# An MLP in two parts of its inner width, squares a step ahead, and two tiles given up, in a four-layer network

## The chip, the cores and the metric

The kernel runs on one core of a Trainium2 chip. The metric is device time in microseconds for one execution, in which the core computes all four layers for the whole batch of 8 images. The time before is the median of three runs, 7783.18 us (7766.74 to 7798.79).

TensorE is called PE in the profile (PEld its weight loads), VectorE is DVE, ScalarE is ACT, GpSimd is POOL, and SyncE is SP, whose queue issues every transfer of this kernel.

## The reference

The input is 8 images of 384 channels and 32 x 32 pixels in float32. Four layers follow each other, and each adds its result to its input, which a group norm (32 groups of 12 channels) has scaled before:

```python
x = x + L0(_gn(x))   # selective scan ("Mamba") over the 1024 pixels
x = x + L1(_gn(x))   # 1x1 conv, 8x8 FFT filter, 3x3 depthwise, gelu gate, 1x1 conv
x = x + L2(_gn(x))   # layer norm, selective scan, then an MLP 384 -> 1536 -> 384
x = x + L3(_gn(x))   # 3x3 depthwise conv
```

The scan is the core of L0 and L2. For 768 inner channels d and 16 states n it runs over the pixels t:

```python
dt = softplus(dt @ dt_proj_w.T + dt_proj_b)
h  = exp(dt_t * A) * h + (dt_t * u_t) * B_t      # for each d and n
y  = sum_n(h * C_t) + u * D
y  = y * silu(z);  out = y @ out_proj_w.T
```

L2 puts a layer norm ahead of the scan and, behind its output projection, `gelu(t @ mlp_w1.T + b1) @ mlp_w2.T + b2`.

## The kernel before

An image is cut into two chunks of T = 512 pixels, so that each scan layer has 16 chunks. A chunk's 768 channels times 16 states are 96 scans of 128 partitions by 512 pixels, taken four at a time: 24 steps a chunk (`QUADS`, channel block k of 6, part sub of 4), 768 steps in all. The main loop walks over the steps. In step t it issues

- `times` (L623): POOL multiplies the tile g of step t + 1 (dt*u, spread over states) by B;
- `scan` (L643 to L660): DVE runs four scans; two end in PSUM and DVE multiplies them by C (L654), two end in g and POOL multiplies them by C (L660);
- `gather` of step t - 1: PE sums over states into y with `sely`. With the last sub of a block it adds u*D (in L0 by a matmul with the diagonal matrix w_D, in L2 by DVE, L678) and multiplies by the gate z (L681);
- `begin` of step t + 3 (L613): SP loads g, 1 MB, from a DRAM copy `dud` of dt*u, once `gather` has freed one of four g tiles;
- `decay` of step t + 1: PE spreads dt over states into the four PSUM tiles dA, and ACT takes their exp (L241).

All other work is cut into pieces (Python generators run by `Jobs`), and it is put between these. `begin` of `Jobs` gives each step a budget of TensorE and VectorE time (`ROOM`), `step` takes pieces by due time while they fit, and `until` forces pieces, in order of due time, until a condition holds. A piece yields NEXT if it goes on in the next step, EARLY if its next piece is to open a step, WAIT if it can't go on. The jobs that matter here:

- `measure`: loads six blocks xk of an image (tile `spm`, two buffers) for the group norm's statistics. `live["spm"]` is True meanwhile.
- `front`: loads xf, normalizes it, in L2 runs `layer_norm`, then the in-projection, the short convolution, dbc, and `step_dt` for six blocks d. `layer_norm` waits until `live["spm"]` is False, and then, k by k in one piece, ACT writes the square sq (tile `spm`) and PE sums it into ps_lv.
- `step_dt`: PE makes ps_dt; ACT makes a softplus part m in tile `spm` by Abs, Exp and Ln; DVE adds it up to dt (L85); a step later POOL multiplies dt by u into tile du (L583, two buffers), and SP spills du into `dud` in four transfers (L590). The loop over d waits while seven dt tiles live or `live["spm"]` is True; a unit that has begun is carried on when the loop comes round.
- `finish`: the output projection, then in L1's place `layer1`, or for L2 the `mlp`, and after the image's second chunk `layer3`.
- `mlp`: for each half of the chunk's pixels (256), `up` makes 12 blocks of the inner width from t, in units of two blocks that share a PSUM tile, Gelu runs over h1, and `down` makes three output blocks, each the sum over all 12. The weights come as pieces of 384 KB (tile mw, four buffers, L889), each loaded for each half, so 24 pieces a chunk. A piece is loaded when a later one is taken.

PE executes in the order of the program: matmuls of jobs, of `gather` and of `decay` share one queue, as all transfers share SP's. The lines L177 (matmul), L241 (activation) and L85 (metered DVE operation) are helpers, so the groups are told apart by tile names.

Of the kernel before, what the change touches and what calls it, by code (L numbers as in the profile page):

```python
# [10 lines left out]
F32 = mybir.dt.float32  # L11
AF = mybir.ActivationFunctionType
ALU = mybir.AluOpType
# [40 lines left out]
def _flat(ap):  # L54
    return ap.rearrange("p a b -> p (a b)")
# [100 lines left out]
def tile_conv_preact_d4(ctx: ExitStack, tc: tile.TileContext, a: dict, out: bass.AP):  # L156
# [10 lines left out]
    live = {"ps": 0, "dt": 0, "x": 0, "spm": False}  # L167
    work = [0.0, 0.0]
    jobs = Jobs(work)
    vector = Meter(nc.vector, work, 1)  # L170
# [182 lines left out]
        vector.tensor_scalar_mul(w["A"], w["A"], -1.0)  # L353
        return w

    def load_diagonal(w, pre):
        w["D"] = wk.tile([P, ND, P], F32, tag="w_D", name="w_D")
        nc.sync.dma_start(w["D"], a[pre + "D"].rearrange("d p q -> p d q"))
# [40 lines left out]
    def measure(s):  # L399

        blocks = [(h, k) for h in range(2) for k in range(KC)]
        loaded = {}

        def load(q):
            if q < len(blocks):
                h, k = blocks[q]
                x = loaded[h, k] = wk.tile([P, T], F32, tag="spm", name="xk", bufs=2)
                nc.sync.dma_start(
                    x, s["src"][s["b"], k * P : (k + 1) * P, h * T : (h + 1) * T]
                )  # L410

        live["spm"] = True
        load(0)
        load(1)
        yield NEXT

        def block(h, k):
            return loaded.pop((h, k)), lambda: load(blocks.index((h, k)) + 2)

        def all_read():  # L420
            live["spm"] = False

        s["stats"] = yield from group_stats(block, all_read, NEXT)

# [35 lines left out]
    def layer_norm(xn):  # L460
        ps = yield from ps_tile("ps_ln")
        for k in range(KC):
            mm(ps, ln_mean, xn[:, k, :], start=k == 0, stop=k == KC - 1)
        for k in range(KC):
            vector.tensor_sub(xn[:, k, :], xn[:, k, :], ps)
        ps_done()
        yield NEXT
        while live["spm"]:
            yield WAIT
        ps = yield from ps_tile("ps_lv")  # L470
        for k in range(KC):
            sq = wk.tile([P, T], F32, tag="spm", name="sq", bufs=2)
            act(sq, xn[:, k, :], AF.Square)
            mm(ps, ln_mean, sq, start=k == 0, stop=k == KC - 1)
        rsqrt(ps, ps, eps_ln)
        yield
        for k in range(KC):
            vector.scalar_tensor_tensor(
                xn[:, k, :], xn[:, k, :], ln_w[:, k : k + 1], ps, ALU.mult, ALU.mult
            )  # L480
        ps_done()
        yield NEXT
        for k in range(KC):
            act(xn[:, k, :], xn[:, k, :], AF.Identity, bias=ln_b[:, k : k + 1])
        yield NEXT

    def front(s):
# [78 lines left out]
        def step_dt(d):  # L566
            got = {}


            def log(ps):  # L570
                mm(ps, w["dt"][DT0:RX, d * P : (d + 1) * P], dbc[DT0:RX, :])
                v = got["m"] = wk.tile([P, T], F32, tag="spm", name="spm", bufs=2)
                act(v, ps, AF.Abs)
                act(v, v, AF.Exp, scale=-1.0)
                act(v, v, AF.Ln, bias=1.0)

            def plus(ps):
                v = s["dt"][d] = wk.tile([P, T], F32, tag="dt", name="dt", bufs=NDT)
                vector.scalar_tensor_tensor(v, ps, 0.0, got["m"], ALU.max, ALU.add)

            def times_u(ps):
                v = got["du"] = wk.tile([P, T], F32, tag="du", name="du", bufs=2)
                nc.gpsimd.tensor_mul(v, s["dt"][d], u[d])  # L583

            def spill(ps):
                to = s["dud"][d] = dram.tile(
                    [NSUB * E8, 4, T], F32, tag="dud", name="dud", bufs=2 * ND
                )
                for j in range(4):
                    nc.sync.dma_start(to[:, j, :], got["du"][32 * j : 32 * (j + 1), :])  # L590

            return [both(log, plus), None, both(times_u, spill)]

        yield from pipe([("ps_bc", [spread(j)]) for j in range(2)])
        yield
        flying = []
        for d in range(ND):
            while live["dt"] >= NDT or live["spm"]:
                yield WAIT
            live["dt"] += 1  # L600

            flying.append(pipe([("ps_dt", step_dt(d))]))
            flying = [f for f in flying if next(f, f) is not f]
            yield NEXT
        while flying:
            flying = [f for f in flying if next(f, f) is not f]
            yield NEXT


    def begin(s, i):  # L610
# [53 lines left out]
    def gather(s, i):  # L664
# [5 lines left out]
        g = s.pop(("g", i))  # L670
        for j in range(4):
            mm(y[32 * j : 32 * (j + 1), :], sely[:, sub, :], g[:, j, :], sub == 0, sub == NSUB - 1 and s["pre"] == "l2_")
        if sub == NSUB - 1:
            u = s["u"][k // NH][:, k % NH, :]
            if s["pre"] == "l0_":
                mm(y, s["w"]["D"][:, k, :], u, start=False)
            else:
                nc.vector.scalar_tensor_tensor(  # L678
                    y, u, s["w"]["vec"][:, k, 4:5], y, ALU.mult, ALU.add
                )  # L680
            nc.vector.tensor_mul(u, y, s["z", k // NH][:, k % NH, :])  # L681
            if k == NH - 1:
                s["half"] = True
# [175 lines left out]
        s["done"] = True  # L859


    TH = T // 2
    NFH = NF // 2
    xp = None

# [6 lines left out]

    def weights():

        parts = [a["l2_mlp_w1"][f : f + 2].rearrange("f p k q -> p f k q") for f in range(0, NF, 2)]
        parts += [
            a["l2_mlp_w2"][m][:, g * NFH : (g + 1) * NFH, :]
            for m in range(KC)
            for g in range(2)
        ]  # L880
        parts = deque(parts + parts)
        loaded = deque()

        def more():
# [11 lines left out]
    def mlp(s):  # L896
        x = s["x"]
        loaded, more = s["weights"]
        first = True

        def take():

            nonlocal first
            if not first:
                more()
            first = False
            return loaded.popleft()

        for half in range(2):
            cols = slice(half * TH, (half + 1) * TH)  # L910
            h1 = p2.tile([P, NF, TH], F32, tag="h1", name="h1")

            def up(f):
                def run(q):
                    def run_q(ps):
                        if q == 0:
                            now[0] = take()
                        cols_q = slice(q * TH, (q + 1) * TH)
                        for k in range(KC):
                            mm(  # L920
                                ps[:, cols_q], now[0][:, q * KC + k, :],
                                s["t"][k][:, cols], start=k == 0, stop=k == KC - 1,
                            )

                    return run_q

                def evict(ps):
                    for q in range(2):
                        act(
                            h1[:, f + q, :], ps[:, q * TH : (q + 1) * TH], AF.Identity,  # L930
                            bias=b1[:, f + q : f + q + 1],
                        )

                now = [None]
                return [run(0), both(run(1), evict)]

            yield from pipe([("ps_up", up(f)) for f in range(0, NF, 2)], deep=1)
            yield EARLY
            for q in range(2):
                part = _flat(h1[:, q * NFH : (q + 1) * NFH, :])  # L940
                act(part, part, AF.Gelu)
            exp_again()
            yield NEXT

            def down(m):
                def sum_up(g, third):
                    def run(ps):
                        if third == 0:
                            now[0] = take()
                        for f in range(third * KC, (third + 1) * KC):  # L950
                            mm(
                                ps[:, :TH], now[0][:, f, :], h1[:, g * NFH + f, :],
                                start=g == 0 and f == 0, stop=g == 1 and f == NFH - 1,
                            )

                    return run

                now = [None]

                def add(ps):  # L960
                    xc = x[:, m, cols]
                    vector.scalar_tensor_tensor(
                        xc, ps[:, :TH], b2[:, m : m + 1], xc, ALU.add, ALU.add
                    )
# [214 lines left out]
```

## Time and profile before

| | us |
|---|---|
| median of three runs | 7783.18 |
| the profiled execution | 7774.96 |
| its span | 7773.2 |
| PE busy | 7244.1 |
| DVE busy | 5787.0 |
| POOL busy | 5638.8 |
| ACT busy | 4034.0 |
| mean granted TensorE clock | 0.922 |

The span is the time from the first to the last instruction of one profiled execution. An engine's busy time counts an instruction from its start to its end, and a matmul that waits or runs at a low clock in between counts as busy too. A row of the groups names the line, the engine, the operation, the tiles written and read, the shape and the count; then come the busy time, the mean of one in ns, and the idle time just before such instructions with what ended it. A row of the waits has the waiting instruction, the one it waited for, the total in us, the number of times and the longest.

The first layer's steps last until about 3552 us, where the first scan of the third layer (the one with the MLP) begins. From about 7590 us on no scan is left, and the last chunk's output projection, MLP and depthwise convolution run alone.

### The profile page before, as it was taken

What the parts mean: (1) busy time and instruction counts of PE and PEld (TensorE: products, weight loads), DVE (VectorE), ACT (ScalarE), POOL (GpSimd) and SP (SyncE); (2) the same over time, 40 slices, a digit from 0 to 9 for tenths busy, and PEclk for the clock granted to TensorE, in tenths of its full rate; (3) what the DMA queues carried; (4) which work ended last, traced back from release to release, by engine and by line L of the source; (5) the groups of instructions that cost most, each with busy time, mean ns of one, the idle gap of its engine ahead of it and who ended that gap; (6) DMA issues with size and microseconds to landing.
All of it is one profiled execution on the core that took longest, in us unless ns stands there. A gap on an engine that the chain in (4) does not pass through costs nothing. (4 is left out here: it accounts for less than half of the span.)

```text
span 7773.2 us, 76689 instructions
## 1 busy us (share of the span) xinstructions
PE 7244.1 (93%) x25762; PEld 3001.0 (39%) x25762; DVE 5787.0 (74%) x7350; ACT 4034.0 (52%) x6980; POOL 5638.8 (73%) x2710
## 2 busy tenths in 40 slices
PE   7989999999999999999999989999999999999998
PEld 2223333333333333333334434444444444444445
DVE  5988788888777878778746765767777677776871
ACT  4445555554554555455545544555555555555543
POOL 5888878788787878778646764767767677676770
PEclk8888889999888999988899999999999999999999
DMA  5666556556565646556536654666656666565662
GB/s 141 141 151 144 138 134 142 136 135 150 127 146 127 141 120 148 128 139 146 129 78 167 174 135 120 165 156 172 165 150 174 155 170 164 149 164 146 171 168 67
DMA packets 288919, 1122.50 MB, mean 144 GB/s; under 512 B 37386, under 2 KB 90970, under 8 KB 190220
## 3 DMA queue, kind: packets, MB, share of 16 engines
q1 hardware_dynamic: 288524, 1117.59, 58.4%
q8 instruction: 204, 3.34, 0.2%
q14 instruction: 191, 1.56, 0.1%
HBM read 1041.96 MB, written 75.50 MB: 144 GB/s over the span
## 5 line engine op out<-in xcount | busy, mean ns | idle before, releaser
L623 POOL TENSOR_TENSOR g<-g,bc 128x1024 f32<-128x1024 f32 x1536 | 3586.8, 2358 | 197.2 <-DMA g<-dud 181.2
L660 POOL TENSOR_TENSOR g<-g,bc 128x1024 f32<-128x1024 f32 x768 | 1806.2, 2352 | 1441.1 <-DVE carry L656 806.6
L241 ACT ACTIVATE dA<-dA,w_A 128x512 f32<-128x512 f32 x3072 | 1860.7, 662 | 1543.3 <-PE dA L177 1530.1
L177 PE MATMUL dA<-dt,selr 32*128 32x512 f32 x6144 | 1573.3, 677 | 70.6 <-DVE g L654 61.9
L643 DVE TENSOR_TENSOR_SCAN dA<-dA,carry,g 128x512 f32<-128x512 f32 x768 | 986.6, 1285 | 616.0 <-issue 275.6
L643 DVE TENSOR_TENSOR_SCAN dA<-dA,g 128x512 f32<-128x512 f32 x768 | 940.6, 1225 | 477.5 <-issue 167.7
L654 DVE TENSOR_TENSOR g<-dA,bc 128x512 f32<-128x512 f32 x1536 | 1053.9, 686 | 29.8 <-DVE dA L643 0.5
L177 PE MATMUL y<-g,sely 128*32 128x512 f32 x6144 | 934.1, 637 | 43.0 <-POOL g L660 37.5
L643 DVE TENSOR_TENSOR_SCAN g<-dA,carry,g 128x512 f32<-128x512 f32 x768 | 940.6, 1267 | 0.0
L643 DVE TENSOR_TENSOR_SCAN g<-dA,g 128x512 f32<-128x512 f32 x768 | 893.3, 1204 | 0.0
L177 PEld LDWEIGHTS dA<-dt,selr 32*128 32x128 f32 x6144 | 470.2, 191 | 984.4 <-DVE g L643 517.3
L177 PE MATMUL ps_dn<-h,mw 128*128 128x256 f32 x2304 | 573.9, 401 | 75.3 <-DMA mw<-in_l_mlp_w 58.6
L177 PE MATMUL ps_up<-t,mw 128*128 128x256 f32 x2304 | 566.8, 394 | 59.0 <-DMA mw<-in_l_mlp_w 44.2
L177 PE MATMUL ps_z<-xf,w_in 128*128 128x512 f32 x1152 | 586.1, 649 | 27.3 <-DVE dt L85 23.6
L177 PE MATMUL ps_in<-xf,w_in 128*128 128x512 f32 x1152 | 566.9, 633 | 27.3 <-DVE u L85 25.5
L177 PE MATMUL ps_dw<-tp,diag 96*96 96x512 f32 x1152 | 572.8, 638 | 15.2 <-ACT diag L241 15.2
L177 PE MATMUL ps_out<-u,w_out 128*128 128x512 f32 x1152 | 543.7, 619 | 10.2 <-DVE x L85 10.2
L177 PEld LDWEIGHTS ps_dn<-h,mw 128*128 128x128 f32 x2304 | 439.5, 197 | 277.0 <-issue 118.8
L177 PEld LDWEIGHTS ps_up<-t,mw 128*128 128x128 f32 x2304 | 425.8, 192 | 268.4 <-issue 148.9
L177 PE MATMUL ps_dw<-xp,diag 128*128 128x512 f32 x864 | 407.5, 622 | 42.2 <-ACT diag L241 40.9
L241 ACT ACTIVATE u<-ps_in,w_vec 128x512 f32<-128x512 f32 x192 | 149.4, 778 | 484.2 <-PE ps_in L177 484.2
L177 PEld LDWEIGHTS y<-g,sely 128*32 128x32 f32 x6144 | 134.2, 111 | 648.5 <-issue 461.1
(99 smaller groups left out, 6463.1 us busy)
## 6 DMA issues: line engine op xcount, KB each, us to landing
g<-dud SPq DMA_DIRECT2D x768, 1024.0 KB, 7.1
mw<-in_l_mlp_w SPq DMA_DIRECT2D x384, 384.0 KB, 7.4
dud<-du SPq DMA_DIRECT2D x768, 64.0 KB, 1.7
xk<-in_x SPq DMA_DIRECT2D x48, 256.0 KB, 4.2
xf<-in_x SPq DMA_DIRECT2D x16, 768.0 KB, 8.4
x<-in_x SPq DMA_DIRECT2D x16, 768.0 KB, 8.5
x_mid<-x SPq DMA_DIRECT2D x16, 768.0 KB, 4.6
xk<-x_mid SPq DMA_DIRECT2D x48, 256.0 KB, 5.0
```

Source lines behind the costliest of these rows:

```text
L177: nc.tensor.matmul(out_, lhsT, rhs, start=start, stop=stop)
L241: nc.scalar.activation(out_, in_, func, **kw)
L623: nc.gpsimd.tensor_mul(g, g, s["bc"][:, 0, :].unsqueeze(1).to_broadcast([P, 2, T]))
L643: nc.vector.tensor_tensor_scan(dAs[j] if j < own else g[:, j, :], dAs[j], g[:, j, :], 0.0 if s["c"] == 0 else carry[:, q : q + 1], ALU.mul ...
L654: nc.vector.tensor_mul(g[:, j, :], dAs[j], s["bc"][:, 1, :])
L660: nc.gpsimd.tensor_mul(g, g, s["bc"][:, 1, :].unsqueeze(1).to_broadcast([P, 4 - own, T]))
```

## The change

Four edits are made.

The MLP no longer halves the pixels. It takes all 512 pixels and halves the inner width: for each half g of the 12 blocks, `up` makes six blocks, Gelu runs over them, and `down` adds their part to each of the three output blocks (with the bias for g = 0, without it for g = 1). Each weight piece is loaded once a chunk, so 12 pieces, in the order in which they are used.

Layer norm's three squares are written by ACT into three `spm` tiles, and the matmuls that sum them come in a later piece, behind a NEXT.

dt*u is written over the softplus tile m. The tile du is gone, and `spm` has three buffers. `live["spm"]` now names its user ("measure", "squares" or "dt"), `measure` waits for its turn as the others do, and the loop over d is rewritten: a unit that has begun is carried on in the next step whether or not the next can begin.

The matrices w_D are not loaded. One step ahead of its matmul, ACT makes each 128 x 128 diagonal from the unit matrix `eye` and the vector D.

```diff
@@ measure
-        live["spm"] = True
+        while live["spm"]:
+            yield WAIT
+        live["spm"] = "measure"
         load(0)
         load(1)
@@ layer_norm
+        live["spm"] = "squares"
+        sq = [wk.tile([P, T], F32, tag="spm", name="sq", bufs=3) for _ in range(KC)]
+        for k in range(KC):
+            act(sq[k], xn[:, k, :], AF.Square)
+        yield NEXT
         ps = yield from ps_tile("ps_lv")
         for k in range(KC):
-            sq = wk.tile([P, T], F32, tag="spm", name="sq", bufs=2)
-            act(sq, xn[:, k, :], AF.Square)
-            mm(ps, ln_mean, sq, start=k == 0, stop=k == KC - 1)
+            mm(ps, ln_mean, sq[k], start=k == 0, stop=k == KC - 1)
+        live["spm"] = None
@@ step_dt
             def times_u(ps):
-                v = got["du"] = wk.tile([P, T], F32, tag="du", name="du", bufs=2)
-                nc.gpsimd.tensor_mul(v, s["dt"][d], u[d])
+                nc.gpsimd.tensor_mul(got["m"], s["dt"][d], u[d])
...
-                    nc.sync.dma_start(to[:, j, :], got["du"][32 * j : 32 * (j + 1), :])
+                    nc.sync.dma_start(to[:, j, :], got["m"][32 * j : 32 * (j + 1), :])
@@ front
-        flying = []
-        for d in range(ND):
-            while live["dt"] >= NDT or live["spm"]:
-                yield WAIT
-            live["dt"] += 1
-
-            flying.append(pipe([("ps_dt", step_dt(d))]))
-            flying = [f for f in flying if next(f, f) is not f]
-            yield NEXT
-        while flying:
-            flying = [f for f in flying if next(f, f) is not f]
-            yield NEXT
+        flying, d = [], 0
+        while d < ND or flying:
+            went = bool(flying)
+
+            if d < ND and live["dt"] < NDT and live["spm"] in (None, "dt"):
+                went = True
+                live["dt"] += 1
+                live["spm"] = "dt"
+                flying.append(pipe([("ps_dt", step_dt(d))]))
+                d += 1
+            flying = [f for f in flying if next(f, f) is not f]
+            if went and not flying:
+                live["spm"] = None
+            yield NEXT if went else WAIT
@@ gather
+        if sub == NSUB - 2 and s["pre"] == "l0_":
+
+            s["D", k] = wk.tile([P, P], F32, tag="D", name="D")
+            act(s["D", k], eye, AF.Copy, scale=s["w"]["vec"][:, k, 4:5])
...
-                mm(y, s["w"]["D"][:, k, :], u, start=False)
+                mm(y, s.pop(("D", k)), u, start=False)
@@ weights
-        parts = deque(parts + parts)
+        parts = deque()
+        for g in range(2):
+            for f in range(g * NFH, (g + 1) * NFH, 2):
+                parts.append(a["l2_mlp_w1"][f : f + 2].rearrange("f p k q -> p f k q"))
+            for m in range(KC):
+                parts.append(a["l2_mlp_w2"][m][:, g * NFH : (g + 1) * NFH, :])
@@ mlp
-        for half in range(2):
-            cols = slice(half * TH, (half + 1) * TH)
-            h1 = p2.tile([P, NF, TH], F32, tag="h1", name="h1")
+        for g in range(2):
+            h1 = p2.tile([P, NFH, T], F32, tag="h1", name="h1")
...
+                        mm(
+                            ps, now[0][:, f % 2 * KC + k, :], s["t"][k], start=k == 0,
+                            stop=k == KC - 1,
+                        )
...
-                return [run(0), both(run(1), evict)]
+                return [run(0), run(1), both(run(2), evict)]
...
+                        mm(ps, now[0][:, f, :], h1[:, f, :], start=f == 0, stop=f == NFH - 1)
...
+                    if g == 0:
+                        vector.scalar_tensor_tensor(
+                            xm, ps, b2[:, m : m + 1], xm, ALU.add, ALU.add
+                        )
+                    else:
+                        vector.tensor_add(xm, ps, xm)
...
-                return [sum_up(0, 0), sum_up(0, 1), sum_up(1, 0), both(sum_up(1, 1), add)]
+                return [sum_up(f) for f in range(NFH - 1)] + [both(sum_up(NFH - 1), add)]
@@ the start
-    load_diagonal(layer_w["l0_"], "l0_")
```

More of the change, by code (lines that the diff above doesn't have):

```diff
@@ L165, in tile_conv_preact_d4 @@
     psy = ctx.enter_context(tc.tile_pool(name="psy", bufs=1, space=PSUM))
-    live = {"ps": 0, "dt": 0, "x": 0, "spm": False}
+    live = {"ps": 0, "dt": 0, "x": 0, "spm": None}
     work = [0.0, 0.0]
@@ L354, in load_mamba @@
         return w
-    def load_diagonal(w, pre):
-        w["D"] = wk.tile([P, ND, P], F32, tag="w_D", name="w_D")
-        nc.sync.dma_start(w["D"], a[pre + "D"].rearrange("d p q -> p d q"))
     def load_out(w, pre):
@@ L406, in load @@
                 h, k = blocks[q]
-                x = loaded[h, k] = wk.tile([P, T], F32, tag="spm", name="xk", bufs=2)
+                x = loaded[h, k] = wk.tile([P, T], F32, tag="spm", name="xk", bufs=3)
                 nc.sync.dma_start(
@@ L420, in all_read @@
         def all_read():
-            live["spm"] = False
+            live["spm"] = None
         s["stats"] = yield from group_stats(block, all_read, NEXT)
@@ L571, in log @@
                 mm(ps, w["dt"][DT0:RX, d * P : (d + 1) * P], dbc[DT0:RX, :])
-                v = got["m"] = wk.tile([P, T], F32, tag="spm", name="spm", bufs=2)
+                v = got["m"] = wk.tile([P, T], F32, tag="spm", name="spm", bufs=3)
                 act(v, ps, AF.Abs)
@@ L595, in front @@
         yield
-        flying = []
-        for d in range(ND):
-            while live["dt"] >= NDT or live["spm"]:
-                yield WAIT
-            live["dt"] += 1
-            flying.append(pipe([("ps_dt", step_dt(d))]))
+        flying, d = [], 0
[7 more added lines that the diff above has]
+                d += 1
             flying = [f for f in flying if next(f, f) is not f]
-            yield NEXT
-        while flying:
-            flying = [f for f in flying if next(f, f) is not f]
-            yield NEXT
+            if went and not flying:
+                live["spm"] = None
+            yield NEXT if went else WAIT
     def begin(s, i):
@@ L859, in layer1 @@
         s["done"] = True
-    TH = T // 2
     NFH = NF // 2
@@ L873, in weights @@
     def weights():
[L875 to L880, printed above, removed]
-        parts = deque(parts + parts)
+        parts = deque()
[4 more added lines that the diff above has]
+                parts.append(a["l2_mlp_w2"][m][:, g * NFH : (g + 1) * NFH, :])
         loaded = deque()
@@ L898, in mlp @@
         loaded, more = s["weights"]
-        first = True
+        now = [None]
         def take():
-            nonlocal first
-            if not first:
+            if now[0] is not None:
                 more()
-            first = False
-            return loaded.popleft()
-        for half in range(2):
-            cols = slice(half * TH, (half + 1) * TH)
-            h1 = p2.tile([P, NF, TH], F32, tag="h1", name="h1")
-            def up(f):
[L914 to L925, printed above, removed]
-                def evict(ps):
[L928 to L934, printed above, removed]
-                return [run(0), both(run(1), evict)]
-            yield from pipe([("ps_up", up(f)) for f in range(0, NF, 2)], deep=1)
@@ new lines, in take, with run, run_k @@
+            now[0] = loaded.popleft()
+        for g in range(2):
+            h1 = p2.tile([P, NFH, T], F32, tag="h1", name="h1")
+            def up(f):
+                def run(k):
+                    def run_k(ps):
+                        if f % 2 == 0 and k == 0:
+                            take()
+                        mm(
+                            ps, now[0][:, f % 2 * KC + k, :], s["t"][k], start=k == 0,
+                            stop=k == KC - 1,
+                        )
+                    return run_k
+                def evict(ps):
+                    act(
+                        h1[:, f, :], ps, AF.Identity,
+                        bias=b1[:, g * NFH + f : g * NFH + f + 1],
+                    )
+                return [run(0), run(1), both(run(2), evict)]
+            yield from pipe([("ps_up", up(f)) for f in range(NFH)], deep=1)
@@ L938, in mlp @@
             yield EARLY
             for q in range(2):
-                part = _flat(h1[:, q * NFH : (q + 1) * NFH, :])
+                part = _flat(h1[:, q * KC : (q + 1) * KC, :])
                 act(part, part, AF.Gelu)
@@ L945, in down, with sum_up @@
             def down(m):
-                def sum_up(g, third):
+                def sum_up(f):
                     def run(ps):
[L948 to L954, printed above, removed]
+                        if f == 0:
+                            take()
+                        mm(ps, now[0][:, f, :], h1[:, f, :], start=f == 0, stop=f == NFH - 1)
                     return run
-                now = [None]
                 def add(ps):
[L961 to L964, printed above, removed]
-                return [sum_up(0, 0), sum_up(0, 1), sum_up(1, 0), both(sum_up(1, 1), add)]
+                    xm = x[:, m, :]
+                    if g == 0:
+                        vector.scalar_tensor_tensor(
+                            xm, ps, b2[:, m : m + 1], xm, ALU.add, ALU.add
+                        )
+                    else:
+                        vector.tensor_add(xm, ps, xm)
+                return [sum_up(f) for f in range(NFH - 1)] + [both(sum_up(NFH - 1), add)]
             yield from pipe([("ps_dn", down(m)) for m in range(KC)], deep=1)
```

## The prediction

> **What bounds the kernel now.** I read the page's first part, the by-form groups, then the waits of PE between 4124 and 7370 us (the second layer's steady part), then one slow step.
>
> ```profile
> span 7773.2 us, 76689 instructions
> PE 7244.1 (93%) x25762; PEld 3001.0 (39%) x25762; DVE 5787.0 (74%) x7350; ACT 4034.0 (52%) x6980; POOL 5638.8 (73%) x2710
> ...
> L177 PE MATMUL ps_dn<-h,mw 128*128 128x256 f32 x2304 | 573.9, 401 | 75.3 <-DMA mw<-in_l_mlp_w 58.6
> L177 PE MATMUL ps_up<-t,mw 128*128 128x256 f32 x2304 | 566.8, 394 | 59.0 <-DMA mw<-in_l_mlp_w 44.2
> ...
> mw<-in_l_mlp_w SPq DMA_DIRECT2D x384, 384.0 KB, 7.4
> ```
>
> PE is the engine nearest its limit, and the MLP's two groups wait for their weights. The waits of that stretch:
>
> ```profile
> PE ps_dn L177 <- DMA mw<-in_l_mlp_w: 58.6, 24, 5.6
> PE ps_up L177 <- DMA mw<-in_l_mlp_w: 44.2, 34, 4.8
> PE ps_dw L177 <- ACT diag L241: 34.6, 12, 4.6
> PE ps_lv L177 <- ACT sq L241: 34.4, 12, 3.0
> ```
>
> So 103 us of PE's idle time there are weights that have not landed, 34 us are layer norm's squares. One step with such waits, in order of time:
>
> ```profile
> 5428.87 1.56 PE L177 MATMUL ps_dn<-h,mw 128*128 128x256 f32 x6
> ...
> 5432.62 1.56 PE L177 MATMUL ps_dn<-h,mw 128*128 128x256 f32 x6 [2.19 <-DMA mw<-in_l_mlp_w]
> ...
> 5438.39 2.83 PE L177 MATMUL ps_dn<-h,mw 128*128 128x256 f32 x12 [1.71 <-DMA mw<-in_l_mlp_w]
> ...
> 5443.05 1.29 DVE L643 TENSOR_TENSOR_SCAN dA<-dA,carry,g 128x512 f32<-128x512 f32 x1 [5.86 <-ACT dA L241]
> ```
>
> PE's queue is in order: the decay matmuls (dA) stand behind the late MLP matmuls, so the next scan starts 5.86 us late. The table by stretch shows the DMA engines full in such steps (busy share 1.00, 254 GB/s in 5429.6 to 5443.1); in the layer norm step (5497.3 to 5509.7) the granted clock is 0.86:
>
> ```profile
> 5429.60:5443.10 13.50, 9.59 (x48) 5.97 (x47) 6.77 (x8) 2.44 (x5) 12.07 (x6) 1.00 1.00 254
> 5497.30:5509.70 12.40, 10.21 (x38) 5.13 (x39) 9.66 (x12) 6.18 (x12) 9.04 (x5) 0.86 0.28 63
> ```
>
> The columns are PE, PEld, DVE, ACT, POOL busy, then clock, DMA share, GB/s. A step without such waits takes 8.9 to 9.0 us (5635.0 to 5652.9, PE busy throughout).
>
> **What the Trainium skill says.** "TensorE: Matmul & The Clock Gate", Back-to-back issue gap, gives a warm gap of N / 2.4 + 2.5 ns, so two matmuls of 256 columns cost almost what one of 512 does. The trace agrees: 72 records of 256 columns take 15.79 us without a wait at the end (0.217 each), 36 of 512 take 15.72 (0.432). The same page, What's actually happening, has PE fall to half its clock after an idle window of about 3.4 us; the 0.86 above agrees. "DMA: Bandwidth & Descriptors", Issuing engines are not separate DMA queues, says all transfers interleave on the same 16 engines; the trace has the weights landing 7.4 us after issue beside the 1 MB g loads, which supports it.
>
> **The change part by part.**
>
> *MLP in two parts of the inner width.* Removed: 192 of 384 weight transfers of 384 KB, 75 MB of 1122 (the built program has 192). Matmuls: 4608 records of 256 columns become 2304 of 512, 4608 x 0.217 = 1000 against 2304 x 0.432 = 995 us: equal. Halved weight loads were hidden (190 ns under 217). In the program's order a full down step now has 8 matmuls, 1.33 weight pieces, where it had 15, 2.5 pieces. With its g load that is 1024 + 512 KB in about 9.4 us, 167 GB/s, against 1024 + 960 KB in 8.9, 228 GB/s: from near the 254 at which the engines were full to well under it. A piece now feeds 5.2 us of matmuls and three pieces lie ahead of the running one, 15.6 us, about the longest landing (16.2). So I take 90% of the waits away: -93 us. At least 50 (start of each MLP, pieces queued behind g loads), at most 103 and 10 more of half clock. ScalarE evicts 192 tiles of 512 for 384 of 256 (474 ns): at about 0.69 us each (a 512-wide eviction with bias took 683 to 778), no longer in total, hidden at 52% busy. VectorE adds: per chunk 6 x 0.472 = 2.83 us become 3 x 0.744 + 3 x 0.68 = 4.27, over 16 chunks +23; a third of it in steps where VectorE sets the end: +8 (0 to +23). The two Gelu passes stay the same size, and the bare MLP at the end keeps its two waits of 3.72 us.
>
> *Fewer transfers beside the others.* In 4124 to 7590 POOL waits 97 us for g loads, and ACT 33 us for xf from x_mid. Both should shrink with the weights; POOL has slack in most steps: -25 (0 to -60).
>
> *Squares a step ahead.* The step's first lv matmul waited up to 3.01 us behind ACT, and PE was at half clock around most of the 16: summing the clock records within 7 us of each lv gives 68 us at half clock in the second layer, 34 lost, beside 34 of idle. The most is -68. But the step also holds the norm's VectorE work (9.66 busy of 12.4), so it cannot shrink much below 10: 2.5 us x 16 = -40 (-20 to -68). The sum's matmuls come a step later, and with them the in-projection; the first unit of dt still stands two steps ahead of the first g load that reads it.
>
> *dt*u over the softplus tile.* POOL's multiply (1.27 us) and the four spills stay. Now the tile is free only when its spill has landed, and ACT's Abs of the third unit after waits for that; behind it in ACT's queue stand the exps of the next step. From the start times of the 192 units, Abs to the last spill's issue is 19.9 us in the median, plus 1.7 to land, and three units later is some 27 us on. The margin is negative only for three units of the start (2 to 3 us each); the least elsewhere is 0.6 us and a tenth lie under 4. I take +8: 3 to 5 at the start, the rest scattered (0 to +60). A unit that waited for room in dt is now carried on in the next step and not only when the next unit starts; in the first layer that moves one multiply and its four spills per chunk some four steps earlier past POOL's and SP's other work: the same work, 0 (-5 to +5). While a lock is held for dt, the measuring of the next image waits a piece; SP's xk loads stand in the same places of the first layer: 0.
>
> *D's diagonals.* 96 activations of 128x128, 400 ns by the like diag row, 38 us on ACT. Each stands a step before its matmul, after the decay exps, where ACT is idle waiting for PE (1530 us in all): +3 (0 to +38). The 384 KB load of w_D leaves the start: up to -2.
>
> *Forced work.* Every second chunk has a step in which the depthwise pieces run at once until the gates are ready; 30 ps_dw and 6 ps_z matmuls become 18 and 3, the rest goes to lighter steps. PE's sum is equal, but VectorE and POOL idle less: -6 (0 to -45).
>
> Sum: -93 + 8 - 25 - 40 + 8 + 3 - 6 = -145. The profiled execution took 7774.96 us (span 7773.2), so 7630. The median shown is 7783, 8 above; I leave this 0.1% out of the size of the gain and predict 7635.
>
> **The rivals.**
>
> *PE is fed through.* PE's stalls in the steady part are 229 us (3246.0 less 3017.1 busy), and about 273 us of its clock records are at half speed, 137 lost. If the weights gone also quiet the clock and the g loads, 103 + 68 + 45 of the burst + 50 of loads and clock = 266: about 7510. For it: the full DMA share in just those steps. Against: the steps have a floor, VectorE's 6.5 us of scans and products plus copies, POOL's 7.05.
>
> *The waits only change their name.* VectorE and POOL become the limit of the steps that were late, and the removed idle comes back as PE waiting for scan tiles; only the largest waits count, -30: 7750. For it: 806.6 us of POOL waiting for VectorE's carry copies. Against: the quiet steps run at 8.9 with PE full.
>
> *ACT is held by the spills.* One mechanism: the Abs of a unit waits for the spill three units before, four units in each of 32 chunks, because SP stands at an earlier g load when the multiply ends. It decides from a mean wait of about 1.2 us over 128 units (150 us, what the rest gains); at 2.5 us it gives 320 - 145 = +175: about 7950. For it: margins under 4 us for a tenth of the units. Against: none below zero after the start.
>
> *It doesn't halve the transfers* is excluded by the built order.
>
> **How the numbers follow.** The forecast 0.62, PE fed through 0.17, waits renamed 0.13, ACT held 0.08. What this kernel's measurement can tell from no change is about 0.5%, 39 us: 7744 to 7822. Waits renamed lies half on each side of that bound. Faster 0.62 + 0.17 + 0.05 = 0.84, same 0.09, slower 0.07. The range from 7510 to 7745 holds the forecast's own 7560 to 7715, most of the fed-through case and half of the renamed one.
>
> **What would show it.** mw x192 and PE waiting under 20 us for it; ps_lv without a wait for sq, its mean under 750 ns; no DMA share of 1.00 in a down step; POOL's wait for g loads in the second half under 75; the first scan of the second layer within 15 us of where it is now (3552 us). Wrong it would be if the Abs rows wait for dud, or if PE's waits for DVE g grow by what the weights' waits lose.

## The result, and the profile after

The changed kernel takes 7805.37 us in the median (7795.43 to 7823.63, 15 runs) where the kernel before took 7785.33 beside it (7746.6 to 7805.42, 15 runs): a ratio of 1.0028, with a 95% interval from 1.0017 to 1.004. It is 0.28% slower, a small difference, but one that the interval tells from none, where 1.9% faster was predicted.

The lines of its page that answer to those shown of before:

```profile
span 7804.3 us, 71854 instructions
...
PE 7263.5 (93%) x23458; PEld 2564.9 (33%) x23458; DVE 5807.1 (74%) x7350; ACT 4025.4 (52%) x6884; POOL 5635.6 (72%) x2710
...
L177 PE MATMUL ps_up<-t,mw 128*128 128x512 f32 x1152 | 579.0, 638 | 83.0 <-DVE dt L85 43.9
...
mw<-in_l_mlp_w SPq DMA_DIRECT2D x192, 384.0 KB, 6.7
```

The change does what it says: half the weight transfers, and no wait for a weight is left. Yet ps_up stands idle for 83 us now, 59 before, and what ends the idle time is DVE. The waits of PE in the steady part of the second scan layer (4124 to 7400 us), after:

```profile
PE ps_in L177 <- DVE u L85: 52.5, 20, 5.0
PE ps_up L177 <- DVE dt L85: 43.9, 12, 5.8
PE ps_dw L177 <- ACT diag L241: 33.0, 7, 5.5
PE ps_up L177 <- ACT h L241: 31.3, 12, 3.0
PE ps_dt L177 <- ACT z L241: 13.3, 7, 1.9
```

The 103 us of weights and the 34 us of squares are gone. In their place stand waits for evictions. PSUM is the memory into which matmuls sum; all jobs share three of its banks, and a bank is free again when another engine has read the finished sum out of it, which is called an eviction. The in-projection and MLP's `up` wait until DVE has added u or dt, or ACT has written h, out of a bank. The first two of these rows in the same stretch before:

```profile
PE ps_in L177 <- DVE u L85: 17.8, 27, 3.8
PE ps_up L177 <- DVE dt L85: 5.5, 7, 1.6
```

Where in an image does the time go? Two chunks of 24 steps make an image. While the scans of an image's second chunk run, the front of the next image's first chunk is made; these 24 steps are called a first chunk below, after that front, and the next 24 a second chunk. The first chunk of steps 552 to 575 in the table by stretch (columns as in the prediction), before:

```profile
5421.40:5652.90 231.50, 212.56 (x906) 106.94 (x906) 180.00 (x197) 124.43 (x204) 177.00 (x85) 0.99 0.70 176
```

and the same 24 steps after:

```profile
5415.90:5680.20 264.30, 236.21 (x752) 82.34 (x751) 183.93 (x200) 128.20 (x206) 176.99 (x84) 0.90 0.53 131
```

It is 32.8 us longer, with less DMA. PE idles 28.1 us instead of 18.9, and the granted clock is 0.90 instead of 0.99, so that some 53 us run at half speed, half of it lost. By the clock records the 32.8 us are 9.2 us of idle time and 23.9 us lost at half clock (27.3 against 3.4). PE's busy time reckoned at full clock is 208.9 us after and 209.2 before, so it is not that more work came into these steps. The second chunk that follows went the other way, 249.3 to 235.9 us: its forced step (579) takes 23.9 us instead of 35.4. Up to step 456, which is the first scan layer and the beginning of the second, there is nothing to find: 4266 us from the first scan on before, 4271 after.

The twelve chunks of steps 456 to 743 together, before and after:

```profile
4361.30:7370.20 3008.90, 2796.42 (x10944) 1331.41 (x10944) 2189.91 (x2805) 1610.41 (x2671) 2116.07 (x1013) 0.96 0.63 159
4361.10:7407.90 3046.80, 2826.97 (x9154) 997.27 (x9153) 2215.54 (x2806) 1582.50 (x2521) 2113.47 (x1012) 0.93 0.55 137
```

Although 137 us of waits were taken away, PE's idle time (length less busy) is 219.8 us after and 212.5 before: as much came back. The time at half clock grew from 249 to 405 us.

The timeline after shows what holds PE in that first chunk (start, length, instruction, and in brackets the idle time ahead of it; each float32 matmul leaves two records, so x6 is three matmuls):

```profile
5504.93 2.74 PE L177 MATMUL ps_dw<-xp,diag 128*128 128x512 f32 x6
...
5535.93 2.45 DVE L646 TENSOR_TENSOR_SCAN g<-dA,carry,g 128x512 f32<-128x512 f32 x2
5538.30 1.51 DVE L85 SCALAR_TENSOR_TENSOR u<-ps_in,w_vec,u 128x511 f32<-128x511 f32 x2
5539.95 5.04 PE L177 MATMUL ps_in<-xf,w_in 128*128 128x512 f32 x6 [4.95 <-DVE u L85]
...
5588.58 0.67 DVE L85 SCALAR_TENSOR_TENSOR dt<-ps_dt,spm 128x512 f32<-128x512 f32 x1
5589.30 2.07 PE L177 MATMUL ps_up<-t,mw 128*128 128x512 f32 x2 [5.81 <-DVE dt L85]
...
5628.33 2.84 PE L177 MATMUL ps_dw<-xp,diag 128*128 128x512 f32 x6
...
5637.71 5.49 PE L177 MATMUL ps_dw<-xp,diag 128*128 128x512 f32 x6 [5.54 <-ACT diag L241]
...
5643.24 0.69 DVE L85 TENSOR_TENSOR acc<-ps_dw,x 128x512 f32<-128x512 f32 x1 [5.15 <-PE ps_dw L177]
```

At 5504.93 the last layer's depthwise convolution begins a tile: three of its nine matmuls. The other six follow at 5628 and 5638, and the tile is evicted at 5643, 138 us later. All that time it keeps one of the three PSUM banks that every job shares. Between, the in-projection and dt each keep up to two banks in flight, because DVE's eviction stands in DVE's queue behind four scans, and the MLP needs one too. With a bank fewer, PE's next matmul waits for that eviction (4.95 and 5.81 us), and after such a pause it runs at half clock: the six records of ps_in take 5.04 us, three matmuls that took 2.84 us one block earlier. (The 5.54 us ahead of the tile's last matmuls are a wait for ACT to make diagonals, not for a bank; before has one of 4.6 us in the same steps.)

So this is theory A: *a depthwise tile begun early is left half done, and the bank it holds is missing where two other pipes need it.* A depthwise piece is three taps (of nine), and the last layer has the latest due time. Where a step has room for one piece and then the front and the MLP, due earlier, take all room for ten steps, the tile stays open. In the kernel before no depthwise tile of the last layer was open across the in-projection; what changed is only which steps have some room left.

Theory B: the finer MLP pieces (three matmuls to a PSUM tile instead of six half-wide ones, evicted twice as wide) crowd the in-projection and dt by themselves, whoever holds a bank. Theory C is the prediction's own rival, ScalarE held by spills. The trace leaves nothing of it; the one wait of that kind in all of after:

```profile
ACT spm L241 <- DMA dud<-spm: 1.6, 1, 1.6
```

### The profile page after: what moved, and what is told of

Its sections match the earlier page's. It is cut to its first block, busy times and chain, and to the rows that moved or that the text cites. A ratio compares the mean times of both kernels' runs of the same rounds, so it can differ in the third digit from the quotient of the medians.

```text
span 7804.3 us, 71854 instructions
## 1 busy us (share of the span) xinstructions
PE 7263.5 (93%) x23458; PEld 2564.9 (33%) x23458; DVE 5807.1 (74%) x7350; ACT 4025.4 (52%) x6884; POOL 5635.6 (72%) x2710
## 5 line engine op out<-in xcount | busy, mean ns | idle before, releaser
L177 PE MATMUL dA<-dt,selr 32*128 32x512 f32 x6144 | 1532.1, 681 | 70.0 <-DVE g L657 61.5
L177 PE MATMUL y<-g,sely 128*32 128x512 f32 x6144 | 954.3, 649 | 63.3 <-POOL g L663 59.5
L177 PE MATMUL ps_up<-t,mw 128*128 128x512 f32 x1152 | 579.0, 638 | 83.0 <-DVE dt L85 43.9
L177 PE MATMUL ps_z<-xf,w_in 128*128 128x512 f32 x1152 | 609.0, 670 | 37.6 <-DVE dt L85 29.4
L177 PE MATMUL ps_in<-xf,w_in 128*128 128x512 f32 x1152 | 585.4, 650 | 62.0 <-DVE u L85 60.3
L177 PE MATMUL ps_dn<-h,mw 128*128 128x512 f32 x1152 | 570.2, 636 | 24.6 <-DVE dt L85 11.6
L85 DVE SCALAR_TENSOR_TENSOR u<-ps_in,w_vec,u 128x511 f32<-128x511 f32 (+1 forms) x384 | 282.0, 745 | 130.0 <-ACT xt L241 101.6
L177 PEld LDWEIGHTS ps_up<-t,mw 128*128 128x128 f32 x1152 | 215.8, 201 | 446.8 <-issue 332.1
```

The source lines that it names most:

```text
L85: return call(out_, *args, **kw)
L177: nc.tensor.matmul(out_, lhsT, rhs, start=start, stop=stop)
```

## The experiments

Twelve kernels ran, in three groups, each beside the kernel before on the same chip. "Hold" below means what the built order of instructions shows, a PSUM tile begun and not evicted for a number of steps; durations of chunks are from the start times of the scans.

**after_gate.** The changed kernel, and the last layer's depthwise convolution waits for a later front.

```diff
+                while s["n"] + 3 < len(chunks) and len(chunks[s["n"] + 3].get("dud", ())) < ND:
+                    yield WAIT
                 yield from depthwise(p2, P, [(dw3[:, k, :], window, take)])
```

> The changed kernel, but the last layer's depthwise convolution of an image doesn't begin before the dt loop of the chunk in flight is through (it was begun with three matmuls, kept its PSUM bank half done for ten steps, and was then gone on with). Theory A, one of three PSUM banks is held by that half done tile while in-projection, dt and MLP share two: the steps of 14 to 17 us in the first chunk of each image go, some 30 us for each of six or seven images, so about 7620, and PE's waits for DVE u, DVE dt and ACT h fall below half. Theory B, the MLP's thirds of a block are laid so that they crowd the in-projection and dt whatever bank is held: within 30 us of 7805. Theory C, the softplus tile waits for its spill: within 30 us of 7805.

Measured: 7719.22 us, ratio 0.9914 (0.9892 to 0.9936). The waits of ps_in and ps_up for u and dt fell from 52.5 and 43.9 us to 5.7 and 14.5, that of ps_up for h from 31.3 to 1.7. The direction is A's, the size half; B and C, which expected no change, are further off.

**mlp_alone.** Of the change, the MLP in two parts only.

Its diff is that of `weights` and `mlp` above.

> The kernel before with the MLP's part of the change alone. In its program too a depthwise tile is held over nine steps in five images. Theory A: what the weights' waits give (about 100 us) is eaten by five holds of some 30 us: 7730 to 7830. Theory B: the same. Theory C (the spill costs): no spill over the softplus tile here, so about 7690.

Measured: 7801.45 us, ratio 1.0025 (1.0011 to 1.0039). Here too a depthwise tile is held, nine steps in five images, and the first chunks of these images take 254 to 260 us (before: 231 to 239). A and B can both live with that; C, which asked for about 7690, cannot.

**mlp_gate.** Both of these edits.

> The MLP's part alone, with the depthwise convolution begun only when the dt loop in flight is through. Theory A: 100 to 170 us faster than the kernel before, 7610 to 7690, and 80 or more under the MLP's part alone. Theory B: as slow as the MLP's part alone, within 30 us.

Measured: 7808.13 us, ratio 1.0034 (1.002 to 1.0048). A's number is missed by 120 us. First chunks did fall to 229 to 237 us, but second chunks, 242 to 248 us in mlp_alone, rose to between 267 and 290. The table by stretch shows why; three successive steps, 596 to 598:

```profile
5812.70:5820.60 7.90, 7.90 (x30) 2.96 (x29) 7.61 (x11) 2.95 (x6) 7.26 (x4) 1.00 0.92 248
5820.60:5864.70 44.10, 39.66 (x100) 13.83 (x98) 16.61 (x24) 19.08 (x26) 10.54 (x11) 0.92 0.20 63
5864.70:5871.00 6.30, 4.53 (x12) 1.57 (x8) 6.20 (x10) 2.50 (x5) 4.21 (x2) 0.50 0.55 138
```

The depthwise work came late and took the room of the next front, whose whole in-projection, dbc and first dt were then forced within one step (`until`, because the next g load needs them). PE works through these 44 us, but DVE is busy for 16.6 and POOL for 10.5 of them, and in the step after PE has too little to do and stands at clock 0.50. The gate in the changed kernel has four such steps of 48 to 55 us as well, and two of 30 and 45; between them its two chunks 600 to 647 take 226.6 and 226.4 us. So a gate frees the bank and can lose it all again in forced bursts: A needed a second sentence.

**before_pin.** The kernel before, where one bank is taken on purpose from the start of the in-projection to the end of dt, in first chunks only.

```diff
+        pin = None
+        if s["pre"] == "l2_" and c == 0 and n >= 20:
+            pin = yield from ps_tile("ps_pin")
+            mm(pin[:, 0:1], eye, eye[:, 0:1])
         yield from pipe(
             ("ps_in", [both(project(s, d, 0), tap(d), taps(d))]) for d in range(ND)
         )
...
+        if pin is not None:
+            act(wk.tile([P, 1], F32, tag="pin", name="pin"), pin[:, 0:1], AF.Copy)
+            ps_done()
```

> The kernel before, with one PSUM bank taken from the in-projection to the end of the dt loop in the first chunk of five images (one matmul of a column writes it, one copy reads it at the end). Theory A: 20 to 40 us for each image, so 100 to 200 slower than before, with PE waiting for DVE u and DVE dt. Theory B or C: within 30 us of before.

Measured: 8105.51 us, ratio 1.0415 (1.038 to 1.045), about twice what A expected. The waits of PE between 4124 and 7400 us:

```profile
PE ps_in L177 <- DVE u L85: 95.1, 41, 4.9
PE ps_dn L177 <- DVE dt L85: 66.1, 12, 6.5
PE ps_up L177 <- ACT h L241: 55.2, 22, 7.3
```

These are the rows that the change brought in, larger. The held bank alone makes them, with the MLP's coarse pieces. The trace has the pin in six images, not in five as expected (n is 20 to 30), and their first chunks are 313 us longer than before, some 52 us each. That it is 52 and not 33 fits a point of the built order, though no run tests it: in the kernel before, the MLP's own ps_up tile stays open for four steps over the same in-projection, so the pin leaves one bank.

The second group took the bursts away too. The flag of **after_flow** says that a front is under way (from its normalization to its last dt), and a depthwise tile of the last layer is not begun while it is (the second condition leaves out the case in which the front itself must wait for that work); the room of a step in this layer grows a little, so that work is not put off until it is forced.

```diff
-ROOM = {"l0_": (5.2, 3.0), "turn": (6.4, 3.0), "l2_": (6.4, 3.0)}
+ROOM = {"l0_": (5.2, 3.0), "turn": (6.4, 3.0), "l2_": (6.8, 3.0)}
@@ depthwise
             if t == 0:
+                while rows == P and live["front"] and "x" in chunks[live["front"]["n"] - 2]:
+                    yield WAIT
                 ps = yield from ps_tile("ps_dw")
@@ front
+        live["front"] = s
         yield NEXT
         for k in range(KC):
...
+        live["front"] = None
```

> The changed kernel with two edits to the order of its work: a tile of the last layer's depthwise convolution is begun only while no front stands between its layer norm and its last dt (a flag set by front), and the room of a step for TensorE in the second Mamba layer is 6.8 instead of 6.4. In the order so built no PSUM bank of the three is held by a half-done tile for more than 3 steps, and no step between 456 and 744 has more than 15 matmuls of planned work. Theory A (a bank held half done is what ate the gain, and the first gate recovered only half because the delayed work came back in forced bursts): each pair of chunks near the one undisturbed pair of the first gate's run (600 to 648: 453 us where the changed kernel has 498), six pairs, so about -270: 7535 us, between 7480 and 7620. Theory B (finer MLP pieces crowd the in-projection and dt, whoever holds a bank): no better than the first gate, 7700 to 7800.

Measured: 7556.37 us, ratio 0.9708 (0.9685 to 0.973), within A's range. The chunk that took 264.3 us:

```profile
5314.90:5542.90 228.00, 223.90 (x767) 80.74 (x766) 182.53 (x199) 135.03 (x203) 179.42 (x86) 0.98 0.61 151
```

PE idles 4.1 us in it instead of 28.1. Its in-projection in the timeline, with the MLP's `down` between as before:

```profile
5429.35 2.84 PE L177 MATMUL ps_in<-xf,w_in 128*128 128x512 f32 x6
5430.86 2.45 DVE L650 TENSOR_TENSOR_SCAN g<-dA,carry,g 128x512 f32<-128x512 f32 x2
5432.03 2.74 PE L177 MATMUL ps_dn<-h,mw 128*128 128x512 f32 x6
...
5433.23 1.51 DVE L85 SCALAR_TENSOR_TENSOR u<-ps_in,w_vec,u 128x511 f32<-128x511 f32 x2
...
5435.77 2.84 PE L177 MATMUL ps_in<-xf,w_in 128*128 128x512 f32 x6
```

The eviction of u still stands behind the scans, but PE has a third bank to work in meanwhile, and ps_in goes on at full clock with no bracket behind it. The fine MLP pieces are those of the changed kernel, so theory B falls.

**before_flow.** The same two edits on the kernel before (here the flag falls when the last dt is begun, a little earlier than in after_flow).

> The same two edits on the kernel before: the price of the change with the bank question taken out of both. Theory A: before keeps its waits for MLP weights (about 100 us), for squares (34 us) and its dud transfers, and loses only its own short holds and bursts, so 7650 to 7760, and the changed kernel with the same edits stands 100 to 150 us below it, near the -145 of the sum on record. Theory B: both with the edits within 30 us of each other, or the one with the coarse MLP pieces ahead.

Measured: 7816.62 us, ratio 1.0032 (1.0016 to 1.0048). Its own range is missed by 57 us: without its bursts and short holds the kernel before does not get faster at all. The distance to after_flow, 260 us, is more than expected. Its waits say what is left in it:

```profile
PE ps_dn L177 <- DMA mw<-in_l_mlp_w: 67.6, 24, 5.3
PE ps_up L177 <- DMA mw<-in_l_mlp_w: 51.1, 28, 4.2
PE ps_lv L177 <- ACT sq L241: 45.0, 13, 9.4
```

That is 164 us of just what the change takes away. Twelve chunks, steps 456 to 743, in the table by stretch, before_flow:

```profile
4396.90:7430.80 3033.90, 2794.25 (x10945) 1336.66 (x10943) 2193.30 (x2814) 1602.59 (x2676) 2121.10 (x1016) 0.95 0.62 158
```

and after_flow:

```profile
4385.20:7164.10 2778.90, 2704.06 (x9139) 966.24 (x9138) 2213.26 (x2804) 1582.89 (x2525) 2119.36 (x1016) 0.97 0.61 151
```

PE's idle time (length less busy) falls from 239.7 to 74.8 us, by 165, and its busy time by 90, of which 75 are the half-clock loss (155 us in before_flow, 80 in after_flow, by the clock records).

**sq_d.** The kernel before with the squares a step ahead and D's diagonals by ScalarE, the MLP and dt*u as before. Its edit is the part of the diff for these two, with three `spm` buffers and `measure` waiting for its turn.

> The kernel before with the squares a step ahead and D's diagonals made by ScalarE (the load of D gone); the MLP with its small weight tiles and the three tiles of dt*u as before. Its built order holds a depthwise tile half done for ten steps in five images, as the changed kernel's does, though no MLP piece differs. Theory A: the squares' wait goes (-34) but five held banks come at 25 to 35 us each, so 7860 to 7930, slower than before. Theory B: no finer MLP piece, so no crowding: 7730 to 7770.

Measured: 7990.11 us, ratio 1.0262 (1.0241 to 1.0283), slower still than A said, and 220 us above B's range. No MLP piece differs from before, but a depthwise tile is held for ten steps in five images, and beside it ps_up for four. PE's largest wait in 4124 to 7400 us is

```profile
PE ps_in L177 <- DVE u L85: 81.8, 32, 4.9
```

and the chunk of steps 552 to 575

```profile
5448.20:5723.90 275.70, 228.69 (x868) 108.06 (x867) 181.23 (x198) 129.45 (x217) 179.30 (x85) 0.88 0.57 145
```

So the hold is not the MLP's doing: a layer norm with one piece more also leaves the room at the wrong step.

**mlp_flow.** mlp_alone with the flag; the room stays 6.4.

> The MLP in two parts alone, with the flag that keeps a depthwise tile from being begun under a front; the step's room stays 6.4. In the built order no depthwise tile is held over the in-projection, and the only forced bursts are 36 matmuls once an image (30 in the MLP-alone run). Theory A: the first chunk of an image falls from 255 us to about 230 and the second stays near 245: 7801 - 5 x 25, so 7675, between 7640 and 7720. Theory B: within 20 us of the MLP alone, 7780 to 7820.

Measured: 7679.52 us, ratio 0.9872 (0.985 to 0.9894), 4 us from A's number; first chunks 226 to 230 us. The flag alone turns the MLP in two parts from 0.25% slower to 1.3% faster.

The third group asked what the larger room does without the flag, what the parts are worth, and whether more room is better. **after_room** is the changed kernel with ROOM 6.8 only.

> The changed kernel with the room of a step alone (6.8 instead of 6.4) and without the flag: in its built order a bank is again held half done across the in-projection, a depthwise tile for 9 steps in one image and an out-projection tile for 9 steps in four, and there are no forced bursts in those images. Theory A (it is the held bank, whatever tile holds it): the 7556 us of both edits plus five images at about 35 us, so 7730, between 7690 and 7790. Rival (the larger room is what pays and the flag is nothing): 7530 to 7580.

Measured: 7627.12 us, ratio 0.9793 (0.9776 to 0.9809). It lies between the two ranges, 71 us above after_flow and 178 below the changed kernel. Its own chunks tell why. Steps 504 to 527, with a depthwise tile held over the in-projection and dt, and steps 552 to 575, with an out-projection tile held for nine steps:

```profile
4875.40:5136.10 260.70, 234.07 (x772) 82.71 (x771) 184.34 (x200) 128.92 (x217) 174.67 (x83) 0.93 0.55 136
5375.50:5603.60 228.10, 221.05 (x756) 80.72 (x756) 178.29 (x191) 128.55 (x228) 171.38 (x80) 0.98 0.57 144
```

Within one run, a chunk with one kind of hold takes 260.7 us and one with the other 228.1, as good as without. The out-projection tile is open while depthwise pieces and layer norm's sum run beside it, and it is evicted at 5484.3 us, before the in-projection begins at 5500.7. So A was put too broadly: a held bank costs nothing by itself here. It costs about 33 us an image where it lies over the in-projection and dt.

**no_mlp_flow** and **mlp_flow68** are the change without its MLP, and its MLP alone, both with flag and room.

> Everything of the change but the MLP (squares a step ahead, dt*u over a softplus tile, D's diagonals by ScalarE), with both edits to the order, so that no bank is held. It keeps the small weight tiles and the waits for them (119 us in the run of before with both edits). Expected if the MLP's part is the larger one: 7817 less the squares' 45 and some 20 of TensorE's clock after them, 7750, between 7710 and 7790. If the squares and dt*u are what paid: 7560 to 7640.

Measured: 7791.44 us, ratio 1.0011 (0.9999 to 1.0023). The upper end is passed by 1 us.

> The MLP's part alone with both edits to the order. It keeps the wait of ps_lv for the squares and the separate tiles of dt*u. If the parts add up once no bank is held: 7556 plus what the other parts are worth (some 65), 7620, between 7580 and 7660. If the MLP's part needs the others to pay: 7700 or more.

Measured: 7624.01 us, ratio 0.979 (0.9772 to 0.9809), as expected. With the ratios of the four kernels that have both edits:

| with flag and room | us | to the kernel before |
|---|---|---|
| nothing of the change | 7816.62 | 1.0032 |
| squares, dt*u, D | 7791.44 | 1.0011 |
| the MLP | 7624.01 | 0.979 |
| all of it | 7556.37 | 0.9708 |

The MLP is worth 2.4% alone and 3.0% on top of the others; the others 0.2% alone, which is no more than the intervals, and 0.8% on top of the MLP. In no_mlp_flow PE's waits for squares are gone, but between 4124 and 7400 us ps_z now waits 41.0 us for ACT to evict bc, beside 111 us of waits for weights. Why that wait came in is open.

**after_flow70** has the flag and a room of 7.0.

> The changed kernel with the flag and a room of 7.0 instead of 6.8: no bank held, no bursts, but some steps with more work and a few with next to none. If the room is no longer what decides: within 25 us of 7556. If steps must be filled evenly: 7580 to 7650.

Measured: 7591.67 us, ratio 0.9742 (0.9722 to 0.9763), between the two numbers. More room does not help; 6.8 is not shown to be the best value, only better than 6.4 with a gate and than 7.0.

after_flow is the fastest of all kernels here: 2.9% under the kernel before, 3.2% under the changed one.

## Why the prediction was wrong, by its steps

*The weights, -93.* The mechanism was right: their waits went from 102.8 us to none, as "what would show it" asked. The size was right or too small. With flag and room, the MLP's part takes 2.4%, some 190 us, where the sum has -110 for it (weights, adds and transfers). In steps 456 to 743 mlp_flow68 is 169 us shorter than before_flow: 105 us of idle time, 32 us less lost at half clock, and 32 us of busy time at full clock that no run takes apart. In the changed kernel as it stands about as much is given back.

*VectorE's adds, +8.* No run takes it apart. Waits of PE for DVE x are 12.2 us in after_flow, in two places of the stretch.

*Fewer transfers beside others, -25.* POOL's wait for g loads (4124 to 7590 us) fell from 97.5 us to 41.9. It had slack, and no run shows a gain of its own.

*Squares, -40.* Their wait is gone (a ps_lv record takes 610 ns in the mean of the whole run, 915 before). With the MLP changed and no bank held, squares, dt*u and D together bring 64 us, more than the sum of their three terms (29); without the MLP changed, 16.

*dt\*u over the softplus tile, +8, and D's diagonals, +3.* ACT waits 1.6 us for a spill in the whole run, and the run up to step 456 is as long as before, within 5 us. The rival of a ScalarE held by spills did not come.

*Forced work, -6.* This is the step that failed. It read from the built order that "30 ps_dw and 6 ps_z matmuls become 18 and 3, the rest goes to lighter steps", found PE's sum equal, and took it for a small gain. Part of the rest that went to lighter steps was the depthwise tile begun at 5504.93. The step counted what was moved in PE time. It did not ask what a moved piece keeps while it waits for the next one: a third of the shared PSUM banks, for ten steps, over the in-projection and dt. Its bounds, 0 to -45, excluded a loss. Measured, a hold over these parts costs about 33 us (260.7 against 228.1 us in one run, 264.3 against 228.0 between the changed kernel and after_flow).

Against the kernel before, the six first chunks from step 456 on are 23 to 33 us longer, 173 us together, and all the rest of the run is 142 us shorter (spans 7804.3 and 7773.2); part of that are the forced steps that the term was about, as the one above that fell from 35.4 to 23.9 us. That the rest comes so near to the -145 of the sum is partly luck: the first chunks hold gains too, and single terms were off. The 250 us between the changed kernel and after_flow are more than this loss: 85 of them lie in steps 456 to 503 (556 us and 471), where the kernel before is as slow, 569 us.

None of the rivals had it. "The waits only change their name" comes closest, but it named PE waiting for scan tiles, and put it at -30. The test that was written down, PE's waits for DVE g growing, did not see it; it was DVE u and DVE dt that grew. The signs of being right came true: no PE wait for weights or squares, POOL's wait for g loads at 41.9 us, the second scan layer's first scan 13.6 us later than before, no step with `down` matmuls up to step 743 with a DMA share over 0.87. They tested the gains, and none of them looked at PSUM.

Two readings in the prediction's paragraph on the skill say less than they seem to. The formula of "TensorE: Matmul & The Clock Gate", Back-to-back issue gap, gives, as an estimate, 109 ns for 256 columns where a record takes 217, so it is the ratio of the two widths that agrees, not the size. The clock of 0.86 is one half-clock stretch of 3.4 us beside a pause of 3.01 us, which is shorter than the idle window named there, so it does not show that window (see the last section).

The Trainium skill, "PSUM — Partial Sum Buffer", Specifications (TRN2), gives a core eight banks. The kernel has all of them in use: four for dA, one for y, three shared by the jobs. No run shows the number itself; what the runs show is that PE stands idle for want of one of these three, and the budget of a step does not count them.

Open remains why before_flow does not gain from the loss of its bursts. How the 33 us divide is not the same everywhere: between before and after, the chunk shown has 9.2 us of idle time and 23.9 at half clock; between the two chunks of after_room it is 19.5 us of idle time and 12.1 at half clock.

## What to carry to other kernels

When work is cut into pieces that accumulate in a shared PSUM bank, a piece has two prices: its time and the bank that it keeps until its last partner is done. So after any change that alters where a step has room left, look in the built order for tiles that stay open, and over what they stay open. Begin a long accumulation only where it can end before the part with two evictions in flight, and check that putting it off does not bring it back as forced work.

A wait that is taken away need not show in the total when the same engine then meets another: one and the same edit of the MLP gave -2.4% in the one order and +0.25% in the other.

## What was not expected of the hardware

Short pauses of TensorE cost more than their length. The Trainium skill, "TensorE: Matmul & The Clock Gate", What's actually happening, has half clock follow an idle window of about 3.4 us. In the changed kernel's trace between 4124 and 7400 us all 21 gaps of 4 to 6.5 us between matmuls are followed by half clock within 3.5 us, which agrees. But so are all 11 gaps of 2.5 to 3.2 us (12 of 18 in the kernel before, 6 of 9 in after_flow), so the page's figure is not a lower bound here. The stretches at half clock last 3.41 us or a multiple (6.83, 10.24), so a wait of 3 us can cost another 1.7 to 5 us, half of such a stretch. In each of the three traces all these stretches begin on one grid of 3.41 us. Cut along that grid, every piece at full clock in which matmuls were busy for less than 40% is followed by half clock (25 of 25 before, 21 of 21 in the changed kernel, 7 of 7 in after_flow), and of those busy for over 90% it is 38 of 2255. So it seems to be the busy share of such a piece that counts, and not the length of one pause; that is read from these counts, and no run tests it. (Counted from the clock records and the matmuls' times.)
